# An audio tower on one core: the last 64 tokens of two heads in one tile, and a plan with other shares

## The chip, the cores and the metric

The kernel runs on one core of a Trainium2 chip. A core has a matrix engine (TensorE, PE in the profile; its weight loads are PEld), a vector engine (VectorE, DVE), an engine for functions such as sine and exponential (ScalarE, ACT), a general one (GpSimd, POOL), and SyncE (SP), whose queue issues all the DMAs here. Each engine works through its own list of instructions in order and waits on semaphores. On-chip memory has 128 partitions; matmuls write into PSUM, of 8 banks of 512 fp32 columns. The metric is the device time of one execution in microseconds; lower is better.

## The reference

The input is 32 sequences of 160000 samples, padded and cut into 313 frames of 512. A token is a frame times an orthonormal cosine basis. One layer follows, attention and then a feed-forward part, both on layer-normed tokens and with a residual. All is fp32.

```python
h = einsum('bfh,kh->bfk', frames, D)                       # 32 x 313 x 512
# attention, 8 heads of 64
Q, K = xpos(X W_Q), 1/xpos(X W_K)
p = softmax(Q K^T) * gamma_h ** |n - m|                    # decay by distance
Y = groupnorm_per_head(p V)
h = h + (silu(X W_G) * Y) W_O
# feed-forward: 256 units, 512 features
theta = x[..., None, :] / (1 + |W|) + B                    # 313 x 256 x 512 a sequence
sin, cos = table of 4096 entries at round(theta * 4096 / 2 pi)
h = h + silu(sum_d(cos * a_cos) proj_cos^T + sum_d(sin * a_sin) proj_sin^T)
```

The feed-forward takes a sine and a cosine for each of 32 x 313 x 256 x 512 angles; that is most of the work.

## The kernel before, in words

**Feed-forward.** Sequences come in pairs; `STARTS` gives each of the 16 pairs a round at which it enters, and it stays for 8 rounds of 32 units each (`ffn_round`). A round works on all the pairs that are in it, one at first, then two to four. A slot is 24 strips of 313 tokens (a unit and a block of 128 features, for each sequence of the round). VectorE computes integer indices (L665, one instruction for each unit and block), adds a quarter turn (L674) and masks (L681). ScalarE takes two sines of 7512 elements, the cosine's and the sine's (L689), into two `trig` buffers. TensorE sums over the features with 32-column weights `hot` (L711). One sine is one unit of the plan's key.

**Attention** (`attention`, one sequence at a time, 32 in all). It runs beside the feed-forward of earlier pairs; the first two, in buffers `a` and `b`, run before any sine, and all others use `a`. The 313 tokens stand in three tiles of N = 105 rows that start STEP = 104 rows apart, so one row is in two tiles. The steps are: frames times the cosine basis (`rows`, L303), layer norm (`layernorm`), transposes (L290), values (L303, copied to `v`), and for each of the four pairs of heads g `rotary` (columns L318, products L384, L387) and `scores` (L401, maximum L406, subtraction L410). Rotated queries and keys of two pairs share the buffer `u`. The differences lie in `prob`, 8 heads x 3 tiles x 313 columns. ScalarE takes exponentials of four heads at once (L427) and VectorE sums rows (L442); while no more than one pair is in the rounds, ScalarE does it per tile and head, with the sums (L431). For each head a table of decays is loaded into half of `u` (L450), the probabilities are transposed (L457) and multiplied by decays on the way out of PSUM (L469); for each two heads the product with values follows (L480), copied by L486. Then come the gate (L318, silu L494), the group norm (squares L510, sums L515, reciprocal root on GpSimd, spread by L540), the output product (L303), the residual (L558), a second layer norm and transposes, and the rows are stored in DRAM as `xT_d`, from where the rounds load them.

**Order.** Nothing is ordered by hand: every operation is put into a `Plan` with a key, an engine, a guessed duration, and what it reads and writes. `emit` walks through time; on each engine it takes the ready operation of the lowest key. A slot's indices and sines have the slot's key, its sums on TensorE have `key - 1` (L719), hot loads `key - 4`. An attention's stages have keys spread between its begin and end by `SHARE`, whose entries count once for each time in `TIMES`. Begin and end come from the loop at L849: a pair of attentions must end 8 keys before its round, the first pair 12.

**Places.** `prob` also serves, by its keys `probs`, for the rotary table, its products, the group norm's tables (`of_head`, `head_w`) and residuals; `room` is the first three heads.

Of the kernel before, what the change touches and what calls it, by code (L numbers as in the profile page):

```python
# [21 lines left out]
P = 128  # L22
# [7 lines left out]
SHARE = dict(rows=5.0, copy=2.5, norm=11.0, turn=0.7, rotary=4.2, scores=6.4, exps=1.5, head=3.5,  # L30
             pair=0.8, gate=3.5, silu=0.8, group=7.0, affine=5.0)
# [8 lines left out]
NT = 3  # L40

# [91 lines left out]
def tile_audio_tower(ctx: ExitStack, tc: tile.TileContext, t: dict, out: bass.AP):  # L133
    nc = tc.nc
    n_seq, S = t["frames"].shape[0], t["frames"].shape[3]
    STEP = (S - 1) // NT
    N = S - STEP * (NT - 1)
    assert STEP + 1 == N <= P
    ROW0 = [i * STEP for i in range(NT)]
# [17 lines left out]
    class Buffers:  # L157


        def __init__(self, name, pool, psum):  # L160
# [3 lines left out]
            self.probs = [(name, "prob", a) for a in range(H)]  # L164

            def sb(key, *shape):
# [5 lines left out]
            self.dec = [  # L172
                self.u[:, 2 * i : 2 * i + 2, :].rearrange("p c s -> p (c s)")[
                    :, : STEP * (NT - 1) + S] for i in range(2)]
# [8 lines left out]
            self.prob = sb("prob", H, NT, S)  # L183
            wide = self.prob.rearrange("p a b s -> p (a b s)")
            self.wide = wide


            self.table, self.turn = (
                wide[:, a * NT * S : a * NT * S + 4 * S].rearrange("p (i s) -> p i s", s=S)
                for a in (H - 4, H - 2))  # L190
            self.raw = wide[:, H * NT * S - 2 * S :].rearrange("p (i s) -> p i s", s=S)
            self.room = self.probs[:3]
            self.hres = wide[:, : NT * HOP].rearrange("p (i d) -> p i d", d=HOP)
            self.sqT = wide[:, : NC4 * S].rearrange("p (c s) -> p c s", s=S)
            k = NC4 * S
            self.rT = wide[:H, k : k + S]
            self.of_head = wide[:, k + S : k + S + NC4 * H].rearrange("p (c h) -> p c h", h=H)
            k += S + NC4 * H
            self.head_w = wide[:H, k : k + NC4 * P].rearrange("p (c d) -> p c d", d=P)
            self.mx = [sb(f"mx{i}", 2) for i in range(2)]  # L200
            for key in ("sm", "gv", "gr", "gu"):
                setattr(self, key, sb(key, NT, H))
# [29 lines left out]
    def rsqrt(plan, key, val, r, u, kv, kr, ku, early):  # L232
# [23 lines left out]
        if early:  # L256
            plan.add(key, "DVE", 1600, newton, (kv,), (kr, ku))
        else:
            plan.add(key, "POOL", 13000, patient, (kv,), (kr, ku))
# [25 lines left out]
    def transposed(plan, key, x):  # L285

        for c in range(NC4):
            def go(c=c):
                for i in range(NT):
                    nc.tensor.transpose(  # L290
                        x.W[:, c, ROW0[i] : ROW0[i] + N], x.h[:N, i, c * P : (c + 1) * P],
                        ident[:N, :N],
                    )
            plan.add(key, "PE", 400, go, x.rows_of, x.banks(c))

    def rows(plan, key, x, lhsT, src, r, order=range(NT), src_r=(), banks=(0, 1, 2)):

        for c in range(NC4):
            k = x.load(plan, key, src[c], src_r)
            for to, i in zip(banks, order):  # L300
                plan.add(
                    key, "PE", 970,
                    lambda c=c, i=i, k=k, to=to: nc.tensor.matmul(  # L303
                        x.W[:N, to, :], lhsT[:, c, ROW0[i] : ROW0[i] + N], x.ring[k],
                        start=(c == 0), stop=(c == NC4 - 1)
                    ),
                    (*r, x.k("ring", k)), x.banks(to),
                )
# [14 lines left out]
    def attention(plan, keys, sq, x, eng, swap_m=None):  # L323
# [12 lines left out]
        def residual(key, load):  # L336
            for i in range(NT):
                f0 = 1 if i and not load else 0
                d, s = h_d[sq, ROW0[i] + f0 : ROW0[i] + N, :], x.h[f0:N, i, :]
# [3 lines left out]
                else:  # L343
# [3 lines left out]
        hs, probs, room, us = x.rows_of, x.probs, x.room, x.every("u", 2)  # L347
# [10 lines left out]
        rows(plan, step("rows"), x, x.xnT, wv_d, (x.k("xnT"),), range(NT - 1, -1, -1),  # L358
             ("wv_d",))
        copy(plan, step("copy"), eng, NT * HOP, x.v[:N], W3.rearrange("n j (g d) -> n j g d", d=P),  # L360
             x.banks(0, 1, 2), hs)
        plan.add(step(), "POOL", 2000, lambda: nc.gpsimd.memset(x.v[0:1, : NT - 1], 0.0), (), hs)

        plan.add(step(), "SP", DMA_NS, lambda: nc.sync.dma_start(x.table, t["turn_qk"]),
                 (), probs[-4:-2])

        def rotary(g):
# [8 lines left out]
            else:  # L376
                copy(plan, key, eng, 2 * S, x.raw, x.W[:, 0:2, :S], x.banks(0, 1), probs[-1:])
                for i in range(2):
# [3 lines left out]
                             probs[-1:], x.banks(2 + i))  # L382
            plan.add(key, "DVE", 1500,
                     lambda: nc.vector.tensor_tensor(x.turn, x.W[:, :, :S], x.table, ALU.mult),  # L384
                     (*probs[-4:-2], *x.banks(0, 1, 2, 3)), probs[-2:])
# [3 lines left out]
                     probs[-2:], (kq,))  # L389

        def scores(g):
# [3 lines left out]
            for i in range(NT):  # L395
                b = (g * NT + i) % 2 * 2
                m, km = x.mx[(g * NT + i) % 2], x.k("mx", (g * NT + i) % 2)

                def go(i=i, b=b):
                    for a in range(2):  # L400
                        nc.tensor.matmul(  # L401
                            x.W[:N, b + a, :S], qk[a * DH : a * DH + DH, 0, ROW0[i] : ROW0[i] + N],
                            qk[a * DH : a * DH + DH, 1, :], start=True, stop=True)
                plan.add(key, "PE", 690, go, (kq,), x.banks(b, b + 1))
                plan.add(key, "DVE", 800,
                         lambda b=b, m=m: nc.vector.tensor_reduce(  # L406
                             m[:N], x.W[:N, b : b + 2, :S], AX.X, ALU.max),
                         x.banks(b, b + 1), (km,))
                plan.add(key, "DVE", 810,
                         lambda i=i, b=b, m=m: nc.vector.tensor_tensor(  # L410
                             x.prob[:N, 2 * g : 2 * g + 2, i, :], x.W[:N, b : b + 2, :S],
                             m[:N].unsqueeze(2).to_broadcast((N, 2, S)), ALU.subtract),
                         (km, *x.banks(b, b + 1)), probs[2 * g : 2 * g + 2])


        for half in range(2):
            for g in (2 * half, 2 * half + 1):
                rotary(g)
            for g in (2 * half, 2 * half + 1):
                scores(g)  # L420


        key = step("exps")
        for a0 in (0, H // 2):
            def exps(a0=a0):
# [574 lines left out]
```

## Time and profile before

| | |
|---|---|
| median of 3 runs | 18446.96 us (18434.6 to 18453.94) |
| profiled execution | 18427.45 us |
| its span, first to last instruction | 18425.7 us |
| ScalarE busy | 17817.6 us, 97% |
| VectorE busy | 17099.8 us, 93% |
| TensorE busy, matmuls | 14166.8 us, 77% |
| GpSimd busy | 1268.7 us, 7% |
| granted TensorE clock | 0.92 |

Times inside are from the one profiled execution. A group's line names the source line, the engine and the operation, then out<-in with shapes and the count; after the bar stand its busy time and the mean of one in ns, and after the next bar the idle time of the engine just before it with what ended most of it. A line of waits gives who waited for whom, the total in us, how often, and the longest. A matrix product in fp32 shows as two records.

### The profile page before, as it was taken

The page shows a single profiled execution, that of the slowest core. Times are in us where ns is not written, and L with a number is a line of the kernel's source. Part 1 is how long each engine was busy: PE and PEld are TensorE (multiplying, and loading weights), DVE is VectorE, ACT ScalarE, POOL GpSimd, SP SyncE. Part 2 cuts the span into 40 slices and gives each one's busy share as a digit, 9 for nine tenths or more (in the row PEclk, how much of TensorE's full clock was granted, in tenths as well). Part 3 has the DMA queues.
Part 4 walks back from the last instruction along what each step waited for, and adds up shares of the span by engine and source line. Part 5 has one row for each costly group of instructions (what it writes and reads, how often), then busy time and mean ns, then how long its engine had stood idle before and what let it go on. Part 6 is the DMA issues. An engine that isn't in the chain of part 4 may idle for free. (4 is left out here: it accounts for less than half of the span.)

```text
span 18425.7 us, 322107 instructions
## 1 busy us (share of the span) xinstructions
PE 14166.8 (77%) x146432; PEld 6345.6 (34%) x146432; DVE 17099.8 (93%) x11554; ACT 17817.6 (97%) x3250; POOL 1268.7 (7%) x1118
## 2 busy tenths in 40 slices
PE   7888888777777787777787777877777777766666
PEld 4333334333333333333333333333333333322222
DVE  6999999999999999999999999999998999988888
ACT  4899999999999999999999999999999999999999
POOL 0011111010100010000101000010100000000000
PEclk8999999999999999999999999999999999998888
DMA  3221121111111111111111111111111111110101
GB/s 95 79 67 60 56 67 58 54 48 58 49 39 48 58 50 51 52 44 54 49 56 48 50 46 50 57 51 54 45 43 49 42 52 52 42 43 22 38 26 57
DMA packets 610376, 947.69 MB, mean 51 GB/s; under 512 B 123600, under 2 KB 348880, under 8 KB 598768
## 3 DMA queue, kind: packets, MB, share of 16 engines
q1 hardware_dynamic: 609008, 927.08, 16.4%
q8 instruction: 1148, 18.81, 0.4%
q14 instruction: 220, 1.80, 0.0%
HBM read 822.15 MB, written 104.66 MB: 50 GB/s over the span
## 5 line engine op out<-in xcount | busy, mean ns | idle before, releaser
L689 ACT ACTIVATE trig<-ix 128x7512 f32<-128x7512 int16 (+1 forms) x2758 | 17390.1, 6391 | 319.2 <-PE pa L711 178.8
L711 PE MATMUL pa<-trig,hot 128*32 128x313 f32 x131072 | 10255.2, 466 | 3630.8 <-ACT trig L689 3584.3
L711 PEld LDWEIGHTS pa<-trig,hot 128*32 128x32 f32 x131072 | 4274.7, 118 | 9500.3 <-ACT trig L689 4888.7
L665 DVE TENSOR_SCALAR ix<-xT,f 128x2504 int16<-128x2504 f32 (+3 forms) x5504 | 6531.3, 1247 | 120.0 <-ACT trig L689 58.8
L681 DVE TENSOR_SCALAR ix<-ix 128x15024 int16<-128x15024 int16 (+4 forms) x1655 | 5581.6, 3387 | 39.9
L674 DVE TENSOR_SCALAR ix<-ix 128x7512 int16<-128x7512 int16 (+1 forms) x1379 | 2902.6, 2105 | 646.2 <-ACT trig L689 558.7
L318 PE MATMUL a_W<-a_xnT,a_ring 128*128 128x313 f32 x4896 | 1455.8, 440 | 56.0 <-DVE a_prob L410 13.6
L303 PE MATMUL a_W<-a_ring,a_u 128*105 128x512 f32 x2160 | 1036.6, 618 | 93.4 <-ACT a_h L599 37.6
L318 PEld LDWEIGHTS a_W<-a_xnT,a_ring 128*128 128x128 f32 x4896 | 884.0, 190 | 631.9 <-issue 252.0
L250 POOL TENSOR_TENSOR a_gu<-a_gr 105x24 f32<-105x24 f32 x90 | 118.7, 1318 | 8753.3 <-DVE a_gr L238 8748.6
L303 PEld LDWEIGHTS a_W<-a_ring,a_u 128*105 128x105 f32 x2160 | 347.6, 174 | 661.4 <-issue 567.9
L250 POOL TENSOR_TENSOR a_lu<-a_lr 105x3 f32<-105x3 f32 x180 | 196.2, 1090 | 4870.7 <-DVE a_lr L238 4861.3
L457 PE MATMUL a_W<-ident,a_prob 105*105 105x105 f32 x2232 | 294.3, 276 | 194.7 <-DVE a_prob L469 155.1
L303 PE MATMUL a_W<-a_ring,a_xnT 128*105 128x512 f32 x840 | 399.4, 614 | 16.7 <-ACT a_h L599 6.5
L457 PEld LDWEIGHTS a_W<-ident,a_prob 105*105 105x105 f32 x2232 | 242.0, 180 | 338.5 <-DVE a_prob L469 147.9
L410 DVE TENSOR_TENSOR a_prob<-a_W,a_mx 105x626 f32<-105x626 f32 x372 | 301.2, 810 | 59.7 <-PE a_W L401 36.1
L406 DVE TENSOR_REDUCE a_mx<-a_W 105x2 f32<-105x626 f32 x372 | 298.4, 802 | 43.0 <-PE a_W L401 31.8
L401 PE MATMUL a_W<-a_u 64*105 64x313 f32 x1488 | 260.9, 457 | 80.7 <-DVE a_mx L406 56.3
L469 DVE TENSOR_TENSOR a_prob<-a_W,a_u 105x939 f32<-105x939 f32 x248 | 280.0, 1129 | 25.0 <-PE a_W L457 22.6
L480 PE MATMUL a_W<-a_prob,a_h 105*64 105x313 f32 x1488 | 241.9, 453 | 76.2 <-DVE a_prob L469 76.1
L384 DVE TENSOR_TENSOR a_prob<-a_W,a_prob 128x1252 f32<-128x1252 f32 x124 | 180.7, 1458 | 49.0 <-PE a_W L380 34.5
L442 DVE TENSOR_REDUCE a_sm<-a_prob 105x6 f32<-105x1878 f32 x108 | 220.3, 2101 | 0.0
(144 smaller groups left out, 3452.3 us busy)
## 6 DMA issues: line engine op xcount, KB each, us to landing
hot<-in_hot SPq DMA_DIRECT2D x1376, 128.0 KB
xT<-xT_d SPq DMA_DIRECT2D x80, 1252.0 KB
a_u<-in_decay SPq DMA_DIRECT2D x248, 260.5 KB
xT<-xT_d SPq DMA_DIRECT2D x36, 939.0 KB
a_ring<-in_proj SPq DMA_DIRECT2D x128, 256.0 KB
a_ring<-in_dct SPq DMA_DIRECT2D x124, 256.0 KB
a_ring<-wv_d SPq DMA_DIRECT2D x124, 256.0 KB
a_ring<-in_wq SPq DMA_DIRECT2D x124, 256.0 KB
```

Of the source, the lines that this page charges most:

```text
L250: nc.gpsimd.tensor_tensor(u, r, r, ALU.mult)
L303: lambda c=c, i=i, k=k, to=to: nc.tensor.matmul(x.W[:N, to, :], lhsT[:, c, ROW0[i] : ROW0[i] + N], x.ring[k], start=(c == 0), stop=(c == N ...
L318: lambda c=c: nc.tensor.matmul(x.W[:, bank, :S], w[:, c, :], x.xnT[:, c, :], start=(c == 0), stop=(c == NC4 - 1)),
L406: lambda b=b, m=m: nc.vector.tensor_reduce(m[:N], x.W[:N, b : b + 2, :S], AX.X, ALU.max),
L410: lambda i=i, b=b, m=m: nc.vector.tensor_tensor(x.prob[:N, 2 * g : 2 * g + 2, i, :], x.W[:N, b : b + 2, :S], m[:N].unsqueeze(2).to_broadca ...
L457: nc.tensor.transpose(x.W[:N, jj, ROW0[i] : ROW0[i] + N], x.prob[:N, a, i, ROW0[j] : ROW0[j] + N], ident[:N, :N],)
L469: nc.vector.tensor_tensor(x.prob[:N, a], x.W[:N, :NT, :S], w3, ALU.mult)
L665: nc.vector.tensor_scalar(ix[:, x[0], pt * r * S : (pt + 1) * r * S], now["xT", y][:, : r * S], f[:, 0, n : n + 1], f[:, 1, n : n + 1], AL ...
L674: nc.vector.tensor_scalar(ix[:, x[1], :E], ix[:, x[0], :E], float(LUT // 4), None, ALU.add)
L681: nc.vector.tensor_scalar(ix[:, i, :E], ix[:, i, :E], LUT - 1, LUT // 2, ALU.bitwise_and, ALU.bitwise_xor)
L689: nc.scalar.activation(tl[:, :E], ix[:, x[1 - k], :E], AF.Sin, bias=-PI32, scale=ANG)
L711: nc.tensor.matmul(now["pa", p][g * 32 : g * 32 + 32, :S], now["hot", hot[n // 4 * 4, c]][:, n % 4, k, :], now["trig", w][:, s0 : s0 + S], ...
```

## The change

The 313 tokens now stand in two tiles of 128 rows and one of the last 64; the tiles overlap by 7 rows (`TWICE`). In the last tile the rows of one head stand in partitions 0 to 63 and those of its neighbour in 64 to 127, so that two heads have five tiles in `prob` in place of six. Rows, residuals and values of the last tile are made or loaded twice, once for each half. The last tile's scores are taken for two pairs of heads at once (`last_scores`), and its row sums in one further reduction. Decays of two heads are loaded together, into the whole of `u` or a spare place of four strips, which also holds the rotary table. The last keys' transposes are made by plain matmuls with the identity, two heads side by side. The seven doubled rows of `v` are cleared in both halves. Apart from this, `SHARE` has other numbers, GpSimd's guess is 10000 for 13000, the first pair of attentions is due 13.6 keys ahead for 12.0, and a slot's sums have `key - 2`.

```diff
-SHARE = dict(rows=5.0, copy=2.5, norm=11.0, turn=0.7, rotary=4.2, scores=6.4, exps=1.5, head=3.5,
-             pair=0.8, gate=3.5, silu=0.8, group=7.0, affine=5.0)
+SHARE = dict(rows=5.0, copy=2.5, norm=9.3, turn=1.4, rotary=4.2, scores=7.6, exps=1.2, head=4.2,
+             pair=0.8, gate=2.1, silu=1.3, group=4.9, affine=6.0)
...
+LAST = 64
...
-    STEP = (S - 1) // NT
-    N = S - STEP * (NT - 1)
-    ROW0 = [i * STEP for i in range(NT)]
+    N = P
+    ROW0 = [0, P, S - LAST]
+    TWICE = 2 * P - ROW0[2]
+    WIN = S + P
...
+            wide = sb("prob", (5 * NC4 + 4) * S)
+            self.prob = wide[:, : 5 * NC4 * S].rearrange("p (g x s) -> p g x s", g=NC4, s=S)
+            spare = wide[:, 5 * NC4 * S :]
+            self.dec = [self.u.rearrange("p c s -> p (c s)")[:, : 2 * WIN + S],
+                        spare[:, : 2 * WIN + S]]
...
-            plan.add(key, "POOL", 13000, patient, (kv,), (kr, ku))
+            plan.add(key, "POOL", 10000, patient, (kv,), (kr, ku))
...
+                def go(c=c, i=i, k=k, to=to):
+                    for o in (0,) if i < 2 else (0, LAST):
+                        n = P if i < 2 else LAST
+                        nc.tensor.matmul(
+                            x.W[o : o + n, to, :], lhsT[:, c, ROW0[i] : ROW0[i] + n], x.ring[k],
+                            start=(c == 0), stop=(c == NC4 - 1))
...
-            for i in range(NT):
-                b = (g * NT + i) % 2 * 2
+            for i in range(2):
+                b = turns[0] % 2 * 2
...
+        def last_scores(g):
+            key, b = step(), turns[0] % 2 * 2
+            def go():
+                for y in range(2):
+                    for a in range(2):
+                        r = slice(a * DH, a * DH + DH)
+                        nc.tensor.matmul(x.W[r, b + y, :S], x.qk[y][r, 0, ROW0[2] : S],
+                                         x.qk[y][r, 1, :], start=True, stop=True)
+            plan.add(key, "PE", 1240, go, us, x.banks(b, b + 1))
+            below_max(key, b, x.prob[:, g : g + 2, 4, :], (probs[g][4], probs[g + 1][4]))
...
-                    nc.scalar.activation(x.prob[:N, a0 : a0 + H // 2], x.prob[:N, a0 : a0 + H // 2],
-                                         AF.Exp)
+                    nc.scalar.activation(x.prob[:, g0 : g0 + 2], x.prob[:, g0 : g0 + 2], AF.Exp)
...
+            for g in range(NC4):
+                plan.add(step(), "DVE", 1465,
+                         lambda g=g: nc.vector.tensor_reduce(
+                             sm4[:, :, 2 * g : 2 * g + 2],
+                             x.prob[:, g, 0:4, :].rearrange("p (i h) s -> p i h s", i=2),
+                             AX.X, ALU.add),
+                         probs[g][:4], (x.k("sm", g // 2 * 2),))
+            plan.add(step(), "DVE", 1465,
+                     lambda: nc.vector.tensor_reduce(
+                         x.sm[:, 2 * H :], x.prob[:, :, 4, :], AX.X, ALU.add),
+                     [probs[g][4] for g in range(NC4)], (x.k("sm", 0),))
+        for g in range(NC4):
+            key, d = step("head"), g % 2
+            dec, kd = x.dec[d], us if d == 0 else (x.spare,)
             plan.add(key, "SP", DMA_NS,
+                     lambda g=g, dec=dec: nc.sync.dma_start(dec, t["decay"][g]), (), kd)
...
+                for jj in range(2):
+                    def go(g=g, a=a, jj=jj):
+                        k = slice((1 - jj) * P, (2 - jj) * P)
+                        for i in range(2):
+                            nc.tensor.transpose(x.W[:, jj, i * P : (i + 1) * P],
+                                                x.prob[:, g, 2 * i + a, k], ident)
+                        r = slice(a * LAST, a * LAST + LAST)
+                        nc.tensor.transpose(x.W[:, jj, ROW0[2] : S], x.prob[r, g, 4, k],
+                                            ident[r, r])
...
+                if a == 0:
+                    def both(g=g):
+                        k = slice(ROW0[2], S)
+                        for a in range(2):
+                            r = slice(a * LAST, a * LAST + LAST)
+                            for i in range(2):
+                                nc.tensor.matmul(
+                                    x.W[r, 2, i * P : (i + 1) * P], x.prob[:, g, 2 * i + a, k],
+                                    ident, start=True, stop=True)
+                            nc.tensor.matmul(x.W[r, 2, ROW0[2] : S], x.prob[r, g, 4, k],
+                                             ident[r, r], start=True, stop=True)
+                    plan.add(key, "PE", 600, both, probs[g], x.banks(2))
+                decayed(key, 2, x.prob[:, g, a : a + 3 : 2, :], 0, a * WIN, x.banks(0, 1),
+                        (probs[g][a], probs[g][a + 2]))
+            decayed(key, 1, x.prob[:, g, 4:5, :], 2, 2 * WIN, x.banks(2), (probs[g][4],))
...
-                plan.add(key - 1, "PE", 150 * len(parts) * r, go,
+                plan.add(key - 2, "PE", 150 * len(parts) * r, go,
...
-        due = [(key_of[STARTS[q]] - (8.0 if q > 1 else 12.0) - k) / (q - p + 1) for q in range(p, len(STARTS))]
+        due = [(key_of[STARTS[q]] - (8.0 if q > 1 else 13.6) - k) / (q - p + 1) for q in range(p, len(STARTS))]
```

Here `decayed` multiplies n banks of PSUM from bank b by the decays from column o of the loaded table into their place in `prob`.

## The prediction

> **What bounds the kernel now.** I read the page first: busy times (part 1), then the costliest groups (part 5).
>
> ```profile
> PE 14166.8 (77%) x146432; PEld 6345.6 (34%) x146432; DVE 17099.8 (93%) x11554; ACT 17817.6 (97%) x3250; POOL 1268.7 (7%) x1118
> ...
> L689 ACT ACTIVATE trig<-ix 128x7512 f32<-128x7512 int16 (+1 forms) x2758 | 17390.1, 6391 | 319.2 <-PE pa L711 178.8
> ```
>
> The sines of the feed-forward (L689) fill 17390.1 us of ScalarE, and the diff does not touch their number or shape. All other ScalarE work is 17817.6 - 17390.1 = 427 us; its idle time is 18425.7 - 17817.6 = 608 us. No more than these 1035 us can be won. To place them I asked for busy times in windows cut where rounds with more sequences begin (start up to 306; rounds 0-3; 4-6; 7-8; 9-10; 11-12; 13-14; the last two rounds). A row gives each engine's busy us and its instructions.
>
> ```profile
> core 0: us, PE busy (x) PEld busy (x) DVE busy (x) ACT busy (x) POOL busy (x), PEclk, DMA share, GB/s
> 0.00:306.00 306.00, 228.38 (x846) 123.94 (x846) 146.24 (x242) 51.06 (x124) 2.60 (x8) 0.84 0.36 110
> 306.00:977.00 671.00, 539.65 (x4975) 259.50 (x4976) 634.42 (x768) 587.50 (x201) 44.66 (x74) 0.91 0.26 77
> 977.00:1876.00 899.00, 740.41 (x7194) 343.87 (x7192) 858.83 (x722) 848.33 (x196) 100.85 (x87) 0.92 0.21 63
> 1876.00:2621.00 745.00, 593.96 (x5939) 276.04 (x5940) 717.79 (x542) 702.60 (x121) 79.90 (x61) 0.92 0.20 60
> 2621.00:3497.00 876.00, 711.20 (x7071) 327.25 (x7069) 836.67 (x588) 838.57 (x142) 108.11 (x85) 0.92 0.19 59
> 3497.00:4486.00 989.00, 782.94 (x8096) 357.21 (x8097) 946.75 (x599) 972.82 (x164) 90.58 (x64) 0.93 0.17 51
> 4486.00:5600.00 1114.00, 878.44 (x9166) 392.47 (x9164) 1053.15 (x641) 1107.52 (x186) 92.27 (x86) 0.93 0.16 48
> ...
> 18110.00:18425.00 315.00, 197.90 (x2128) 79.42 (x2128) 253.37 (x289) 274.73 (x48) 0.00 (x0) 0.89 0.15 46
> ```
>
> ScalarE's idle time is 255 us in the start, 83.5 in rounds 0-3, 51, 42 and 37 in the next three stages, 16 in rounds 11-12, then 5 to 7 us in each stage of 1114 us, and 40 at the end. So three regimes: a start where PE (228 of 306 us) and VectorE hand work to each other; rounds 0 to 10, where VectorE is 95 to 96% busy; and from round 13 on ScalarE, over 99% busy. The waits of ScalarE from 306 to 3497 us:
>
> ```profile
> ACT trig L689 <- PE pa L711: 128.3, 73, 6.1
> ACT trig L689 <- DVE ix L681: 69.7, 30, 10.5
> ```
>
> A sine waits for the sums of the sine two before it (two trig buffers) or for its indices. In rounds 0-3 VectorE spends per slot of two sines 12 index instructions (602 ns each by their row, 6.27 us together in the timeline), 2.12 and 4.07: 12.5 us before any attention work, against 12.7 us of sines (6.356 us each, from the spacing of starts). Add attention and VectorE is over-full. There, saved VectorE time is saved time; after round 13 it is not.
>
> **What the Trainium skill says.** "VectorE: DVE Perf Modes", section "Why PSUM operands drop a tier", says that fp32 operands in PSUM go one element a cycle; the trace agrees: 626 elements took 810 ns (L410), 939 took 1129 (L469), 1.02 ns an element, whatever the partitions. "TensorEngine Tiling (Array Packing)", section "Key Properties", says that tiles work in parallel and that a change of tiling mode drains the array. Both are in this trace: 64-column halves (L480) took 241.9/1488 = 0.16 us a record against 1455.8/4896 = 0.30 for whole matmuls of the same 313 columns (L318), and the first record after a change of mode starts 0.354 us after the last, where one of the same mode starts after 0.262: 0.09 us a change.
>
> **The change, part by part.**
>
> *VectorE.* Per attention, scores go from 12 turns to 10: each was 802 + 810 ns, so -3.22 us. Row sums were four of 2101 ns, 8.40 us, and become five over 1252 elements; the nearest row, L384 with 1252 elements, took 1.46, so 7.3: -1.1. Decays were eight of 1129 ns, 9.03 us; they become eight of 626 elements (0.81, L410) and four of 313 (0.48, L486), 8.40: -0.63. The factors' copy grows from 313 to 384 elements: +0.07. Sum -4.9 us; -3.8 in the first five attentions, where ScalarE sums.
>
> *ScalarE.* An exponential of 3756 elements (L427, two an attention, 54 in all) took 3327 ns; the new ones have 3130, and at (3327 - 1191)/(3756 - 1252) = 0.85 ns an element (the 1191 ns from L494) that is -0.53 us each, -1.06 an attention. The first five attentions lose four small ones of 0.45 us each.
>
> *TensorE.* A 64-row last tile forces changes of mode. Per sequence: twelve passes of rows with two changes each, 2.2 us, and four more in the output, 0.7; transposes of layer-normed rows, 16 changes, 1.4; head transposes, 16 groups of two full and one half tile at about 0.46 us against 24 groups of three at 0.28, +0.7; the new group that puts the last tile's transposes of both heads side by side by plain matmuls, four at about 1.2 us, +4.8; other changes +2; scores -0.8. About +11 us, 350 us in all, and TensorE rises from 77 to 79%. It is hidden where ScalarE rules; in the start it is not. With single records in sequence instead of pairs it would be +20 us; the pairs above say 11, which I take.
>
> *DMAs and SP.* Eight decay loads of 260.5 KB become four of 612 KB (1195 columns x 128 x 4 B), +363 KB; residual and output reload the last tile twice, one issue more each. SP issues two fewer per sequence. The page's queue 1 was busy 16.4%. A decay load waits for all of u or for the spare; behind it in SP's queue stand the hot loads that the sums need. Landing of 612 KB has no row: nothing if issued an earlier pair ahead, at most about 5 us at the start's rate of 110 GB/s if bare. I take nothing, as the other pair's work of some 10 us covers it.
>
> *Order.* Sums get a key two, not one, ahead of their sines, so TensorE takes attention's matmuls before them less often; the sums' wait above is what this can touch. Counting, in the order of both built programs, the attention matmuls between one sine's sums and the next with the durations above, rounds 0-3 carry 2.4 us a sine before and 2.7 after, rounds from 11 on 1.4 and 1.5; what gaps hold beyond the 2.9 us that 6.36 - 3.41 leave comes to some 220 us in all before and 330 after; from round 11 on none is longer than a second trig buffer covers (5.9 us). So the earlier key pays for the heavier matmuls; I take both together as zero, between -60 and +60.
>
> *Sum on the profiled execution.* Start: four turns of scores in each interleaved pair at about 2.3 us (starts 98.28, 100.56 in the timeline), -9; TensorE's changes and the plain-matmul transposes on the path, +15; +6. Rounds 0-3: two attentions x 3.8 = -7.6, and the first pair is due 13.6 keys early instead of 12.0 (10 us earlier), against one wait of 12.6 us for its transposed rows at 953 us, half of which I count: -6. Rounds 4-10: five attentions x 4.9 and one x 3.8 = -28.3. Rounds 11-12: two would give -9.8; I take -8, for ScalarE rules then. From 13 on 20 attentions x 1.06 = -21.2 of exponentials, against which I set 1 us more of waits in each of the ten stages for the fuller TensorE, a guess: -11. End: 0. Sum: 6 - 13.6 - 28.3 - 8 - 11 = -55 us. The profiled execution was 18427.45 us around a span of 18425.7, so 18372; the median of the runs lies 19.5 us above it, so 18447 - 55 = 18392.
>
> **Rivals.** *The waits shrink as well.* With the new shares and key the 128 us of waits for sums before 3497 us and 51 us after it fall by half; for it speaks that VectorE has slack of 40 us in each early stage that only such waits explain; against it the counted gaps. Halved, 90 us; but where VectorE rules no more than its own slack returns, so I count 60. Then -55 - 60: about 18332.
>
> *TensorE eats the gain.* In rounds 0-3 it was 540 of 671 us busy and gets 22 more in less time, and in the start it leads. If its 11 us a sequence show in the first twelve attentions at a third, +44: about 18436, no change.
>
> *A wait at each new round, and slower.* At 953 us indices waited 12.6 us for rows that the pair's attention delivered late. The new shares move stages within an attention, gates and norms earlier for fewer keys; if the heavier TensorE makes each of the 14 later pairs late by as much, it costs 176 us: 18392 + 176 = 18568. From five of 14 the gain is gone, from eight it is slower by over 0.2%. Against it: in the built order the last copy of each pair stands 0 to 1 slot earlier against its round than before, and such a wait came once.
>
> That the work doesn't shrink is excluded: 24 tiles of 313 columns become 20.
>
> **From cases to numbers.** Forecast 0.50, with its own range 18360 to 18410; waits shrink 0.16; TensorE eats it 0.22; slower 0.12. 0.2%, 37 us, is about what a measurement of this kernel can tell from no change. Faster by that is 0.66, within it 0.22, slower 0.12. The range leaves out the deepest part of the second case and nearly all of the last: 18320 to 18455.
>
> **What would show it.** Right: 320 reductions and subtractions instead of 384 each at 0.80 and 0.81 us; five row sums of about 1.46; exponentials of 3130 elements at 2.8; the stages of rounds 4 to 10 each 7 to 10 us shorter; a start between 306 and 320 us; TensorE at about 14500 us. Wrong: plain-matmul transposes well over 1.2 us a group, sines waiting over 7 us in a stage of 1114, indices waiting for rows at round starts, or hot loads landing late behind a decay load.

## The result, and the profile after

The changed kernel took 18592.86 us (median; 18579.79 to 18596.51) against 18445.67 us for the kernel before beside it: ratio 1.0079, 95% interval 1.0063 to 1.0095. It is slower by 147 us, where 55 us less were forecast. The profiled execution took 18596.51 us, its span 18594.7; that is 169 us over the profiled span of the kernel before, and it is these 169 us that the stages below divide.

The page of the kernel after, parts 1 and 5:

```profile
PE 14687.0 (79%) x148992; PEld 6446.9 (35%) x148992; DVE 16944.9 (91%) x11581; ACT 17788.9 (96%) x3210; POOL 1132.2 (6%) x1150
...
L749 ACT ACTIVATE trig<-ix 128x7512 f32<-128x7512 int16 (+1 forms) x2758 | 17399.1, 6392 | 489.6 <-PE pa L771 206.8
```

VectorE has 155 us less to do, ScalarE 29 us less, the sines are the same; but ScalarE's idle time before its sines went from 319.2 to 489.6 us. TensorE has 520 us more. Busy times of the kernel after in windows cut at the same rounds as before (start; rounds 0-3; 4-6; 7-8; 9-10; 11-12; 13-14; the last two), each row with a window, its length and each engine's busy us:

```profile
core 0: us, PE busy (x) PEld busy (x) DVE busy (x) ACT busy (x) POOL busy (x), PEclk, DMA share, GB/s
0.00:323.70 323.70, 260.98 (x998) 124.73 (x998) 137.80 (x242) 47.15 (x108) 2.77 (x10) 0.85 0.35 107
323.70:1008.80 685.10, 574.71 (x5126) 267.28 (x5126) 635.78 (x783) 584.49 (x186) 50.51 (x80) 0.91 0.27 79
1008.80:1913.10 904.30, 761.30 (x7370) 348.70 (x7370) 845.89 (x715) 844.28 (x187) 79.24 (x87) 0.93 0.21 63
1913.10:2661.50 748.40, 618.45 (x6045) 279.35 (x6046) 702.60 (x537) 701.19 (x122) 63.10 (x62) 0.92 0.20 61
2661.50:3540.60 879.10, 739.86 (x7228) 331.19 (x7226) 825.97 (x590) 836.23 (x143) 82.36 (x79) 0.93 0.19 60
3540.60:4528.70 988.10, 806.41 (x8242) 360.44 (x8242) 937.29 (x601) 970.55 (x164) 80.30 (x74) 0.94 0.18 53
4528.70:5656.60 1127.90, 911.62 (x9334) 401.24 (x9334) 1043.94 (x647) 1106.74 (x186) 88.93 (x88) 0.93 0.16 49
18273.00:18594.00 321.00, 209.43 (x2144) 80.76 (x2144) 253.29 (x288) 275.25 (x48) 0.00 (x0) 0.85 0.15 45
```

The start is 17.6 us longer, rounds 0 to 12 together 25.1, the eight stages of rounds 13 to 28 together 120.4 (8917.5 to 9037.9), the rest 5.9. Up to round 28 VectorE and ScalarE do less in each stage shown, except VectorE in rounds 0 to 3, and each but rounds 11 and 12 is longer. In rounds 13 to 28 ScalarE's idle time is about 22 us a stage, where it was 4 to 8. So most of the loss lies where ScalarE alone was to rule.

**Who is late there.** A sine waits because the sums that free its `trig` buffer have not been made, so the question is what TensorE did before. Waits of TensorE, kernel before (who waited for whom, us in total, times, longest):

```profile
PE a_W L457 <- DVE a_prob L469: 155.1, 52, 12.7
...
PE a_W L532 <- POOL a_gr L253: 40.1, 13, 5.9
...
PE a_W L303 <- DMA a_u<-in_frames: 28.3, 9, 6.2
```

and kernel after:

```profile
PE a_W L502 <- DVE a_prob L492: 231.8, 95, 9.5
PE a_W L586 <- POOL a_gr L257: 91.2, 26, 5.5
PE a_W L309 <- DMA a_u<-in_frames: 61.0, 13, 7.7
```

The same three hand-offs wait longer: transposes for the decays' product, the transpose of the group norm's factors for GpSimd, and the cosine rows for the loaded frames. For each wait of ScalarE in rounds 13 to 28 I took the longest gap of TensorE in the 16 us before it. Behind those three lay 0.8, 5.8 and 7.7 us of ScalarE's waits before, and 33.1, 54.4 and 39.7 after: 113 of the 129 us by which its waits grew (44 to 173). This goes by nearness in time and proves no cause; the experiments have to.

One such wait, from the timeline of the kernel after (start, us, engine, line and operation; in brackets the idle time before):

```profile
6635.89 2.11 DVE L734 TENSOR_SCALAR ix<-ix 128x7512 int16<-128x7512 int16 x1
6636.13 1.95 POOL L254 TENSOR_TENSOR a_gu<-a_gr 128x20 f32<-128x20 f32 x1 [296.14 <-DVE a_gr L242]
...
6638.04 4.07 DVE L741 TENSOR_SCALAR ix<-ix 128x15024 int16<-128x15024 int16 x1
6638.16 4.03 POOL L255 TENSOR_TENSOR a_gu<-a_gu,a_gv 128x20 f32<-128x20 f32 x1
...
6648.55 0.23 POOL L257 TENSOR_TENSOR a_gr<-a_gr,a_gu 128x20 f32<-128x20 f32 x1
...
6648.84 0.80 PE L586 MATMUL a_W<-ident,a_gr 128*8 128x128 f32 x3 [4.41 <-POOL a_gr L257]
...
6653.38 5.84 PE L771 MATMUL pa<-trig,hot 128*32 128x313 f32 x48
...
6659.35 12.82 ACT L749 ACTIVATE trig<-ix 128x7512 f32<-128x7512 int16 x2 [5.64 <-issue]
```

GpSimd's twelve small steps last 12.65 us (6636.13 to 6648.78); the plan now guesses 10000 ns. So the plan puts L586 ahead of a sine's sums, TensorE stands 4.41 us at its head, with the spreading of the factors and then the sums behind it, and ScalarE stands 5.64. The sums themselves are made mostly while ScalarE waits and take 5.84 us, at a granted clock of 0.57; elsewhere in the same timeline 48 of them take 3.37. The second pattern has a transfer in GpSimd's place:

```profile
6724.97 0.43 SPq L354 DMA_DIRECT2D a_u<-in_frames  x1
...
6732.08 5.33 PE L309 MATMUL a_W<-a_ring,a_u 128*128 128x512 f32 x8 [5.65 <-DMA a_u<-in_frames]
...
6740.82 12.82 ACT L749 ACTIVATE trig<-ix 128x7512 f32<-128x7512 int16 x2 [5.11 <-issue]
```

The first rows come 7.1 us after the issue; the plan has 500 ns for the issue and `LAND`, 2500 ns, for the landing.

### The profile page after: what moved, and what is told of

It is laid out like the page before. It is cut to its first block, busy times and chain, and to the rows that moved or that the text cites. A ratio compares the mean times of both kernels' runs of the same rounds, so it can differ in the third digit from the quotient of the medians.

```text
span 18594.7 us, 327117 instructions
## 1 busy us (share of the span) xinstructions
PE 14687.0 (79%) x148992; PEld 6446.9 (35%) x148992; DVE 16944.9 (91%) x11581; ACT 17788.9 (96%) x3210; POOL 1132.2 (6%) x1150
## 5 line engine op out<-in xcount | busy, mean ns | idle before, releaser
L749 ACT ACTIVATE trig<-ix 128x7512 f32<-128x7512 int16 (+1 forms) x2758 | 17399.1, 6392 | 489.6 <-PE pa L771 206.8
L309 PE MATMUL a_W<-a_ring,a_u 128*64 128x512 f32 (+1 forms) x2880 | 1126.0, 637 | 129.6 <-DMA a_u<-in_frames 61.0
L309 PEld LDWEIGHTS a_W<-a_ring,a_u 128*64 128x64 f32 (+1 forms) x2880 | 321.2, 166 | 800.6 <-issue 714.6
L254 POOL TENSOR_TENSOR a_lu<-a_lr 128x3 f32<-128x3 f32 x180 | 168.4, 935 | 4675.1 <-DVE a_lr L242 4043.9
L309 PE MATMUL a_W<-a_ring,a_xnT 128*128 128x512 f32 (+1 forms) x1120 | 423.2, 623 | 9.8 <-DVE a_xnT L234 3.7
L502 PE MATMUL a_W<-ident,a_prob 128*128 128x128 f32 x992 | 236.8, 324 | 243.0 <-DVE a_prob L492 231.8
L407 DVE TENSOR_TENSOR a_prob<-a_W,a_mx 128x626 f32<-128x626 f32 x310 | 250.9, 809 | 58.9 <-PE a_W L436 26.4
L404 DVE TENSOR_REDUCE a_mx<-a_W 128x2 f32<-128x626 f32 x310 | 248.5, 802 | 32.3 <-PE a_W L436 23.5
L531 PE MATMUL a_W<-a_prob,a_h 128*64 128x313 f32 x1488 | 256.4, 459 | 15.8 <-DVE a_prob L492 15.7
L422 PE MATMUL a_W<-a_u 64*128 64x313 f32 x992 | 174.5, 462 | 56.8 <-DVE a_mx L404 35.1
L309 PEld LDWEIGHTS a_W<-a_ring,a_xnT 128*128 128x128 f32 (+1 forms) x1120 | 123.2, 163 | 261.2 <-issue 235.7
## 6 DMA issues: line engine op xcount, KB each, us to landing
a_prob<-in_decay SPq DMA_DIRECT2D x62, 597.5 KB
a_u<-in_decay SPq DMA_DIRECT2D x62, 597.5 KB
```

Of the source, the lines that this page charges most:

```text
L254: nc.gpsimd.tensor_tensor(u, r, r, ALU.mult)
L309: nc.tensor.matmul(x.W[o : o + n, to, :], lhsT[:, c, ROW0[i] : ROW0[i] + n], x.ring[k], start=(c == 0), stop=(c == NC4 - 1))
L404: lambda: nc.vector.tensor_reduce(m, x.W[:, b : b + 2, :S], AX.X, ALU.max),
L407: lambda: nc.vector.tensor_tensor(place, x.W[:, b : b + 2, :S], m.unsqueeze(2).to_broadcast((P, 2, S)), ALU.subtract),
L502: nc.tensor.transpose(x.W[:, jj, i * P : (i + 1) * P], x.prob[:, g, 2 * i + a, k], ident)
L531: nc.tensor.matmul(x.W[f, 3, :S], x.v[r, jj, g, f], x.prob[r, g, 4 if jj == 2 else 2 * jj + b, :], start=(jj == 0), stop=(jj == NT - 1))
```

## The experiments

The theory: TensorE takes its instructions in the plan's order, and each guessed time that is too short puts an instruction that cannot run yet ahead of a sine's sums. Rivals: TensorE's added work costs by itself; the earlier sums (`key - 2`) or the shares do. The kernel before, run beside each, had medians between 18437 and 18447 us, so I compare ratios; 0.1% is 18 us. Intervals of some 0.15% to either side leave a difference of 0.1% between two runs unresolved.

**Undo single numbers on the new tiles; exchange tiles and numbers.**

```diff
e1_pool13:     -plan.add(key, "POOL", 10000, ...)   +plan.add(key, "POOL", 13000, ...)
e2_key1:       -plan.add(key - 2, "PE", ...)        +plan.add(key - 1, "PE", ...)
e3_tiles_only: after, with the old SHARE, 12.0, POOL 13000, key - 1
e4_plan_only:  before, with the new SHARE, 13.6, POOL 10000, key - 2
```

> The changed kernel with GpSimd's guess for the reciprocal root back at 13000. Theory P (numbers of the plan): the guess of 10000 lets the planner put the factors' transposes on TensorE before GpSimd has ended, which took 12.65 us in the trace; sums stand behind them, and about 54 us of ScalarE's waits from round 13 on and 23 before follow such a wait of TensorE. With 13000 they go to some 17 together: about 18533 us. Theory T (the tiles, with more and other matmuls in TensorE's queue): these waits move to other instructions, 18580 to 18600 us.

> The changed kernel with a slot's sums one key ahead, as before. If the second key does what I took it for, sums ahead of attention's matmuls, taking it back lets more matmuls go before sums: 18600 to 18640 us. If the second key is what delays attention's matmuls and so makes them wait where they hurt: 18540 to 18570 us.

> The new tiles with all the plan's old numbers: shares, GpSimd at 13000, first pair due 12.0 keys ahead, sums one key ahead. Theory P: the tiles alone are worth what I summed, about 55 us, less some 15 us of the start: 18390 to 18430 us. Theory T: the loss comes with the tiles, 18550 us or more.

> The old tiles with all the plan's new numbers. Theory P: the waits for GpSimd come here too, two to four us for each of 30 attentions, 18500 to 18560 us. Theory T: the plan's numbers do little without the new tiles, 18430 to 18470 us.

Measured: e1_pool13 18528.01 us, ratio 1.0047 (1.0032 to 1.0062); e2_key1 18567.99, 1.0069 (1.0052 to 1.0085); e3_tiles_only 18542.81, 1.0055 (1.0040 to 1.0070); e4_plan_only 18511.12, 1.0038 (1.0023 to 1.0053). So GpSimd's guess is worth 0.32%, 59 us, on the new tiles; the second key seems to cost 0.10% there, which these intervals do not resolve; and each half of the change is slower alone: the tiles with none of the new numbers by 0.55%, the numbers on the old tiles by 0.38%. The theory missed e3_tiles_only, for which it gave 18390 to 18430 us: the new tiles lose some 100 us with all the old numbers. In e1_pool13 TensorE's waits for GpSimd fell from 91.2 to 42.6 us:

```profile
L586 PE MATMUL a_W<-ident,a_gr 128*8 128x128 f32 x93 | 17.5, 303 | 42.6 <-POOL a_gr L257 42.6
```

The waits of ScalarE behind GpSimd in rounds 13 to 28 fell from 54.4 to 13.7 us, but all its waits there only from 173 to 150: part of them moved behind other instructions, and more than half of the gain lies before round 13, which begins 32 us earlier.

**GpSimd's guess alone on the old tiles.**

```diff
 before
-            plan.add(key, "POOL", 13000, patient, (kv,), (kr, ku))
+            plan.add(key, "POOL", 10000, patient, (kv,), (kr, ku))
```

> The kernel before with GpSimd's guess at 10000 instead of 13000, nothing else. The new plan numbers all together cost the old tiles 69 us (e4_plan_only). If GpSimd's guess is most of that, as the same edit was worth 65 us on the new tiles, the median lies at 18480 to 18500, with the factors' copy (L532) waiting for GpSimd some 45 us in rounds 13 to 28. If the shares and the key did it, 18440 to 18455.

Measured: 18525.31 us, 1.0043 (1.0028 to 1.0058), some 79 us slower; it is past the upper end of what was expected, and all the loss of e4_plan_only. The group of the factors' transposes of that run (busy, mean ns, idle before and who ended it), 40.1 us of idle in the kernel before:

```profile
L532 PE MATMUL a_W<-ident,a_gr 105*8 105x105 f32 x93 | 16.9, 303 | 89.0 <-POOL a_gr L253 89.0
```

One number of the plan, which changes the order of the instructions and none of them, reproduces the wait on the old tiles. It is not the only one that grew: of ScalarE's waits in rounds 13 to 28, 44 us before and 111 here, 39.0 lie behind GpSimd (5.8 before) and 33.1 behind the frames' load (7.7 before), whose own times in the plan are as they were. So one changed guess also makes waits at other hand-offs. That 13000 is better because it is nearer to the truth is not shown: in the kernel before the twelve steps took over 13 us in 18 of 30 cases, and no run tries a guess above 13000.

**TensorE's own times told.** From the timelines of the kernel after, a group of plain-matmul transposes takes 1.67 us from its first start to the start of what follows it where the plan has 600 ns, and a group of half-tile transposes 0.57 for 400.

```diff
e6_pe_times: e1_pool13 and PE guesses: transposes of probabilities 400 -> 600, plain matmuls 600 -> 1700,
             rows' transposes 400 -> 560, last tile of rows 970 -> 1100, spread 610 -> 900
e8_no_both:  e1_pool13 and, in `both`,   -for i in range(2):   +for i in range(0):
```

> GpSimd at 13000 as in e1, and TensorE's guesses at what the trace of the changed kernel shows: head transposes 600 for 400, the plain-matmul group 1700 for 600, row transposes 560 for 400, the factors' spread 900 for 610, the doubled last tile's rows 1100 for 970. Against e1 at 18528. If TensorE's waits for decays (39 us from round 13 on, 47 before) come from guesses that are too short, some half of them go: 18480 to 18500 us. If they come from VectorE's queue or from the weight of the matmuls themselves: 18520 to 18540.

> GpSimd at 13000 as in e1, and of the group of six plain matmuls that transposes the last tile's keys only the two of 64 columns, so that the last 64 keys of the first 249 queries are left out of the result; the plan is unchanged. It takes some 1.2 us x 4 off TensorE for each attention, 150 us in all. If TensorE's weight is what costs, 18460 to 18500 us against 18528, with a start 5 to 10 us shorter; if it is only the order of waits, 18515 to 18535 and only the start moves.

Measured: e6_pe_times 18481.07 us, 1.0025 (1.0016 to 1.0033); e8_no_both 18462.91, 1.0013 (1.0006 to 1.0020). Against e1_pool13 the measured times are worth 0.22%, 41 us, with the same work; ScalarE's waits behind late decays fell from 39.1 to 18.0 us in rounds 13 to 28. Leaving out four of the six plain matmuls, so that the kernel no longer computes the reference's result, is worth 0.34%, 63 us, and its start is 10 us shorter (315.2 for 325.6). That run does not separate weight from order: the two matmuls that are left take 0.33 us, so the group's guess of 600 ns is no longer too short either.

**The landing told.** First for every DMA, then for the frames alone.

```diff
e7_land5:          e1_pool13 and    -LAND = 2500.0    +LAND = 5000.0
e10_all:           e6_pe_times, LAND = 5000.0 and key - 1
e11_frames:        e6_pe_times and, on the frames' DMA alone,    +late=4500.0 (added to its landing)
e14_before_frames: before and the same late=4500.0
```

> GpSimd at 13000 as in e1, and the planner's time for a DMA's landing 5000 for 2500. From the last copy of an attention to the first matmul of the next one the trace has 11 to 12 us where the plan has about 7, and sums stand behind that matmul. If the plan's landing time is the cause, the 32 us of waits behind that load from round 13 on and 10 before go: 18480 to 18500 us, against 18528. If not, 18520 or more, since later loads make other stages late.

> The new tiles and shares with GpSimd at 13000, TensorE's measured times, landing 5000 and sums one key ahead. If the loss is made of the plan's wrong times, the pieces add up to about 147 - 65 - 30 - 30 - 25 = 0: 18430 to 18470 us. If the tiles themselves cost more than they save, it stays over 18500 us.

> As e6 (GpSimd 13000, TensorE's measured times, 18481 us), and the planner takes 4.5 us more for the landing of the frames alone, so that it counts the 11 to 12 us that the trace shows from an attention's last copy to the next one's first matmul; all other landings stay at 2.5. If that wait costs what stands behind it (36 us from round 13 on, 27 before), 18430 to 18450 us. If, as with a longer landing for all DMAs, a later place for these matmuls makes later stages late: 18480 or more.

> The kernel before, with the frames' landing 4.5 us longer in the plan. Its trace has 8 us of ScalarE's waits from round 13 on behind this load: 18430 to 18445 us, no change that can be told. If the new place costs as much as it saves: up to 18460.

Measured: e7_land5 18743.99 us, 1.0163 (1.0148 to 1.0178); e10_all 18715.82, 1.0147 (1.0130 to 1.0164); e11_frames 18471.54, 1.0016 (1.0009 to 1.0023); e14_before_frames 18402.96, 0.9979 (0.9969 to 0.9988). A longer landing for all loads was a miss: the frames' waits went, but every chain through a load was now planned later (the profile gives no landing times here, so whether 5000 ns is nearer to the other loads than 2500 is not known); the start grew to 335.2 us, rounds 0 to 3 to 714.4, and ScalarE waited some 28 us a stage from round 13. For the frames alone it brought the new tiles less than expected, and the old ones more: there the wait went from 28.3 us to almost nothing, as the group of cosine rows shows (e14_before_frames, columns as above):

```profile
L306 PE MATMUL a_W<-a_ring,a_u 128*105 128x512 f32 x2160 | 1021.5, 611 | 21.7 <-DMA a_ring<-in_dct 15.4 <-DMA a_u<-sums_d 5.6 <-DMA a_u<-in_frames 0.5
```

and six of the eight stages of rounds 13 to 28 took 1109.3 or 1109.4 us, with ScalarE idle for 0.5. This run beats both kernels.

**Key and shares again, where less waits.**

```diff
e12_frames_key1:          e11_frames and key - 1
e13_shares:               e12_frames_key1 with the old SHARE and 12.0
e20_before_frames_key2:   e14_before_frames and key - 2
e21_before_frames_shares: e14_before_frames with the new SHARE and 13.6
```

> As e11, with a slot's sums one key ahead. On the changed kernel one key was 25 us faster than two. If the second key is a cost of its own: 20 to 30 us below e11. If it only moved the waits that e1 and e6 took away: within 10 us of e11.

> As e12, with the old shares and the first pair due 12.0 keys ahead: the new tiles with nothing of the new plan but true times. If the new shares help the new tiles: 10 us or more above e12. If they don't matter: within 10 us of it.

> The kernel before with the frames' landing told (e14_before_frames, 18403), and a slot's sums two keys ahead. If the second key helps wherever the plan's times are true, as in e11_frames against e12_frames_key1, 18380 to 18400, with the gain in rounds 0 to 12; if it costs by itself, as in e1 it would, 18415 to 18435; if it is free without untrue times, 18400 to 18410.

> The kernel before with the frames' landing told (e14_before_frames, 18403), and the new shares with the first pair due 13.6 keys ahead, key - 1 as before. The new shares were set for other tiles: if they cost by themselves, as in e13_shares against e12_frames_key1, 18415 to 18435; if their price lay in the untrue times, 18395 to 18410.

Measured: e12_frames_key1 18492.87 us, 1.0029 (1.0018 to 1.0040); e13_shares 18472.96, 1.0018 (1.0011 to 1.0026); e20_before_frames_key2 18378.04, 0.9967 (0.9954 to 0.9980); e21_before_frames_shares 18437.84, 0.9997 (0.9988 to 1.0005). The second key, if anything a cost in the change as it came, gains 0.13% (24 us) on the new tiles once the plan's times are nearer to the measured ones; there no run with two keys (18448 to 18482 us) is as slow as the fastest with one (18485). On the old tiles, with the frames' landing told, it gains 0.12% (22 us), which the intervals leave open. The new shares cost 0.11% (20 us, at the edge of what the intervals tell) on the new tiles with key - 1, and 0.18% (33 us) on the old; no run here shows them worth anything. The old tiles with the landing told and key - 2 are the fastest of all, 0.33% below the kernel before.

For the change as it came, the steps add up so: of 0.79%, GpSimd's guess is 0.32, TensorE's times 0.22 and the frames' landing 0.09, the last not resolved by the intervals; 0.16%, about 30 us over the kernel before, remain in e11_frames, which keeps the new shares and the second key.

Part 1 of the page of the fastest run, e20_before_frames_key2, against 17817.6 us of ScalarE in a span of 18425.7 before:

```profile
span 18377.1 us, 322162 instructions
## 1 busy us (share of the span) xinstructions
PE 14126.6 (77%) x146432; PEld 6331.4 (34%) x146432; DVE 17097.7 (93%) x11554; ACT 17814.8 (97%) x3250; POOL 1318.5 (7%) x1118
```

The instructions are those of the kernel before, and ScalarE is busy for 2.8 us less in a span that is 48.6 us shorter: nearly all that went is its idle time.

**Is the rest TensorE's weight?** With these times told the new tiles (e11_frames) stay 0.37%, 68 us, above the old (e14_before_frames). Two runs put a weight on the old tiles, one takes some off the new.

```diff
e18b_frames_thrice:      e14_before_frames and   -for i in range(NT):   +for i in (*range(NT), *range(NT), *range(NT)):
e19b_frames_thrice_told: the same and            -plan.add(key, "PE", 400, go, ...   +plan.add(key, "PE", 960, go, ...
e16b_frames_no_both:     e11_frames, the edit of e8_no_both, and 1700 -> 500
```

> The kernel before with the frames' landing told (e14_before_frames, 18403), and every group of three transposes of probabilities made three times over: 24 groups of 0.28 us, twice more, add 13.4 us of TensorE a sequence, 430 us in all, nothing on VectorE or ScalarE; the plan still guesses 400 ns a group. If TensorE's weight is what keeps the new tiles slower, 18440 to 18490, with the start 10 to 20 us longer and 5 to 10 us more of ScalarE's waits in each stage of rounds 13 to 28. If TensorE's weight is hidden and only the order counts, 18395 to 18415.

> As e18b_frames_thrice, with the plan told: 960 ns a group for 400. If the weight costs even when the plan knows it, as in e11_frames, 18430 to 18470; if knowing it lets the plan hide it, 18400 to 18415, and the 68 us of the new tiles are then a matter of order.

> The changed tiles with the plan's times true (e11_frames, 18471.5), and four of the six plain matmuls of each group left out, 500 ns guessed for the group: the products with the last 64 keys of the first 249 queries are left out of the computation, some 1.1 us of TensorE a group, 4.4 us a sequence, 140 us in all. If TensorE's weight keeps the new tiles slower, 18405 to 18440, with the start some 10 us shorter; if it is the order, 18455 to 18475.

Measured: e18b_frames_thrice 18511.77 us, 1.0036 (1.0023 to 1.0049); e19b_frames_thrice_told 18443.24, 0.9999 (0.9990 to 1.0008); e16b_frames_no_both 18418.85, 0.9986 (0.9979 to 0.9992). The added transposes keep TensorE busy for 434 us more by their own line. They cost 0.57%, 105 us, untold, more than expected, and 0.20%, 37 us, told. Taking four of six plain matmuls off the new tiles gains 0.30%, 55 us, for some 143 us of TensorE, within what was expected if weight is the cause. So a microsecond of TensorE's work has no one price here.

Where the told weight costs is seen by stages: round 13 begins 38.6 us later than in e14_before_frames (4536.5 for 4497.9), rounds 13 to 28 last 3.1 us longer, the rest is the same. Windows from 4490 to 13500 us, of e14_before_frames

```profile
4490.00:13500.00 9010.00, 7062.96 (x74316) 3167.54 (x74312) 8543.22 (x5122) 8996.83 (x1508) 744.08 (x605) 0.94 0.16 50
```

of e19b_frames_thrice_told

```profile
4490.00:13500.00 9010.00, 7270.01 (x76556) 3381.29 (x76560) 8546.11 (x5124) 8991.45 (x1509) 703.40 (x604) 0.94 0.17 51
```

and of e11_frames

```profile
4490.00:13500.00 9010.00, 7301.06 (x75230) 3206.49 (x75232) 8423.90 (x5116) 8938.65 (x1502) 728.70 (x620) 0.94 0.16 51
```

ScalarE is idle for 13, 19 and 71 us. A TensorE of nearly the same busy time (7270 and 7301 us) is hidden there in the one plan and not in the other; its instructions are not the same, though.

So the 68 us, 64 in the spans of the profiled executions, have several parts. Before round 13 the new tiles lose only 10.6 us on the old: the weight (39 us for 434 us of work told, so by proportion some 47 for 520, an estimate) would be nearly paid for by VectorE, which is busy for 41 us less in rounds 4 to 12; rounds 7 to 10 are 26.5 us shorter than in e14_before_frames.

In rounds 13 to 28 the new tiles lose 44 us, and 10 after that. For the 44, weight is not the explanation that the runs give: e16b_frames_no_both, whose profiled span is 39.5 us shorter than that of e11_frames, gains 32 us before round 13 and 16 after round 28, and loses 8 between (8934.9 for 8926.9), where ScalarE's waits behind GpSimd came back, 18.6 us for 4.8. What makes those 44 us is open; the gaps of TensorE before them lie at many hand-offs, none above 18 us in total (decays 17.9, the sums before 14.5, rows 9.2).

## Why the prediction was wrong

**The work on VectorE and ScalarE: right.** Groups of the kernel after (busy us, mean ns, idle before):

```profile
L454 ACT ACTIVATE a_prob<-a_prob 128x3130 f32<-128x3130 f32 x54 | 149.0, 2806 | 0.3
```

```profile
L407 DVE TENSOR_TENSOR a_prob<-a_W,a_mx 128x626 f32<-128x626 f32 x310 | 250.9, 809 | 58.9 <-PE a_W L436 26.4 <-PE a_W L422 23.6
L404 DVE TENSOR_REDUCE a_mx<-a_W 128x2 f32<-128x626 f32 x310 | 248.5, 802 | 32.3 <-PE a_W L436 23.5 <-PE a_W L422 8.8
L471 DVE TENSOR_REDUCE a_sm<-a_prob 128x4 f32<-128x1252 f32 x108 | 151.6, 1448 | 0.0
```

With the ten of `b` these are the 320 turns at 0.80 and 0.81 us, row sums at 1.45, exponentials at 2.81. The two attentions of a stage in rounds 13 to 28 took 147.1 us of VectorE before and 137.1 after, 5.0 each for 4.9 forecast, and ScalarE's other work fell by the forecast 2.1 a stage. The decay and hot loads at nothing also held: the sums' waits for hot loads were 1.6 us and are 1.9, and no wait for decays shows. Their growth was mis-summed, though: 260.5 and 612 are in different units; the profile has 597.5 KB a load, so it is 306 KB and not 363.

**TensorE: mechanism right, size off.** 520 us in place of 350. Groups of its transposes:

```profile
L502 PE MATMUL a_W<-ident,a_prob 128*128 128x128 f32 x992 | 236.8, 324 | 243.0 <-DVE a_prob L492 231.8
...
L514 PE MATMUL a_W<-ident,a_prob 128*64 128x128 f32 x992 | 164.7, 289 | 6.6 <-DVE a_h L537 6.6
...
L505 PE MATMUL a_W<-ident,a_prob 64*128 64x64 f32 x496 | 143.4, 289 | 0.5 <-ACT a_prob L458 0.5
...
L517 PE MATMUL a_W<-ident,a_prob 64*64 64x64 f32 x496 | 81.3, 245 | 0.0
```

The plain-matmul group was mis-sized, 1.67 us for 1.2, which is some 60 us in all. The half-tile group took 0.57 us for 0.46, but the old group of three was read too short as well, 0.36 for 0.28 (276 ns is the mean of one record), so their difference about held. The rows came out at 117 us more for 93, and the scores, put at 26 less, at 7 less. In the start this was put at +15 and, less 9 for the scores, at +6; it is +17.6, in which TensorE is busy for 261 us instead of 228.

**The step that failed: "Order. ... I take both together as zero, between -60 and +60."** Two things were wrong in it. It dealt with the key and the heavier matmuls and left out GpSimd's guess, which the diff shows and the sum never priced: it is the largest single item found, 59 us on the new tiles and 79 on the old. And it judged the order by counting which matmuls stand between two sums with their durations, as if each could run when its turn came. An instruction that waits for its input has no such length: with TensorE's measured times told, at the same work and key, 41 us went. So the forecast of rounds 0 to 3, -13.6 us, came out at +14.1, that of rounds 4 to 10, -28.3, at +11.6 (5.5, 3.0 and 3.1), and that from round 13 on, -11, at +126. With measured times in the plan the forecast of rounds 4 to 10 holds in part: rounds 7 to 10 of e11_frames are 29.3 us shorter than in the kernel before, but rounds 4 to 6 still 11.4 longer. The part of the loss that the runs leave open is the 30 us by which e11_frames stays above the kernel before.

**The rivals.** "The waits shrink as well" did not happen here; that the earlier key gains anything was seen only with measured times in the plan. "TensorE eats the gain" came nearest for the tiles: with measured times in the plan they end at 18471.5 us, 36 above its figure, and told weight costs in start and early rounds as it said. "A wait at each new round" has the figure nearest to the measured time, 18568 us, by luck: its wait was not it, since waits of indices for rows fell from 28.5 to 18.0 us. Of the signs named for a wrong forecast two showed, plain-matmul transposes well over 1.2 us a group and sines waiting over 7 us in a stage of 1114 (22); late hot loads and rows at round starts did not.

## What to carry to other kernels

In a kernel whose order is planned from guessed times, price each changed guess as work: compare it with the measured time of that step where it runs, and ask what stands behind the step in its engine's queue. Here the work saved on two engines did not show while TensorE stood before an input that the plan believed to be there. Before rebuilding tiles, tell the plan the times that the trace shows for the few hand-offs that wait: here one such number on the old tiles was worth 0.21%, and with sums one key earlier 0.33%. Tell it hand-off by hand-off and measure each: a longer landing told for all loads at once cost 1.2% on the new tiles.

## What was not expected of the hardware

GpSimd's small steps have no time of their own. In the timeline shown, two of them end 0.08 us after an index instruction of VectorE (6638.00 and 6638.08, 6642.11 and 6642.19) and last 1.95 and 4.03 us; when VectorE has nothing to do, the same steps last 0.2. The twelve together took 6.1 to 15.3 us in the kernel after (mean 12.0) and 7.8 to 20.2 in the one before (14.5), so neither 10000 nor 13000 ns is their time: it depends on what VectorE does beside them. In rounds 13 to 28 of the kernel after they took 12.5 to 12.7 us all 16 times, and TensorE waited for them all 16 times. The Trainium skill, "SBUF — State Buffer", section "Who interferes with whom", says that the two engines share a pair of ports, that VectorE's operations with a scalar operand can enter a two-port mode, and that whichever engine issues first then has the pair for the whole instruction while the other fully blocks. The two pairs of ends agree, and VectorE's instruction starts first in both (6635.89 and 6636.13, 6638.04 and 6638.16); which mode the index instructions run in, no view here shows.

A sine's sums took 3.37 us or up to 6.3, for the same 48 records. "TensorE: Matmul & The Clock Gate", section "What's actually happening", says that the matrix engine's clock is halved after an idle window and comes back after some 3.4 us of work. The trace agrees: 254 of 1341 sums between 4.5 and 13.4 ms took over 4 us before the change, and 267 of 1324 after, and in every one of them the granted clock was at one half for a part of the time (0.66 on average), while nearly all others had the full clock. In the 3.4 us before a slow sum TensorE had stood idle for 2.7 us on average, 2.5 after the change, against 0.9 and 0.8 before the others. So slow sums lengthen each wait, but as there are about as many in both kernels, they do not make the difference.
